# Layer 1 of a two-layer attention kernel: three engines held to the program's order, and the softmax, its bands and the contraction moved one to two columns later

## The chip, the core and the metric

The kernel runs on one NeuronCore of a Trainium2 chip. The metric is the device time of one execution in microseconds, as the median of repeated runs. A profile is one further execution, recorded by the hardware profiler; it is a little longer than the timed ones.

## What is computed

Two layers follow each other on a map of 8 images, 56 rows, 56 columns and 384 channels, all in 32-bit floats. Each adds to its input the result of local attention over 3 x 3 neighbours, after a group normalisation. Layer 1, which the change is about:

```python
a = x_map @ W_attn + b_attn                       # 6 heads x 9 weights for each pixel
a = softmax(a.reshape(B, H*W, heads, k*k), axis=-1)
v = x_map @ W_v + b_v
patches = stack([vp[:, i:i+H, j:j+W, :] for i in range(k) for j in range(k)], axis=3)
y = einsum('bpKhd,bphK->bphd', patches, a)        # weighted sum of 9 neighbours, by head
return y.reshape(B, H, W, C) @ W_proj + b_proj    # and x is added
```

## The kernel before

The images are taken in four pairs. A column is one image column of a pair: 2 x 56 rows, 112 pixels. Seven columns make a group, so that a pair has 8 groups and layer 1 has 32. Layer 0 runs first and takes some 2,340 us; its last tile is finished while layer 1 begins.

Layer 1 is one loop over steps (`layer1`, its loop at L932). Step `g*7 + m` handles column `m` of group `g`, and work of earlier groups beside it:

- `load` (L718) brings the group's input, 1176 KB, from DRAM by a SyncE transfer, into one of four buffers. `normed` (L728) normalises it on ScalarE into `xn`, two sets of 8 columns.
- `attend` (L769) projects 128 pixels at once on TensorE into a PSUM bank (the tiles called "bank"), 54 attention logits and 384 values. VectorE adds the biases: once into `lgt`, once into `v`. ScalarE issues the two stores of `v` to DRAM (`spread`). A tile of 128 pixels straddles two columns of 112, so 8 columns give 7 tiles, and every eighth column (`col % 8 == 0`) has no attend. Below that is a skipped column.
- `regroup` (L792) stores a group's logits to DRAM (`lgtab`, issued by ScalarE) and loads them back with pixels of one column on the partitions (`at`, issued by SyncE).
- `weigh` (L813) is the softmax: maximum and subtraction on VectorE, exp on ScalarE, sum and reciprocal on VectorE, multiplication by the reciprocal on GpSimd (L824).
- `move` (L826) shifts the weights by matrix products on TensorE (`pw`), copies them with nine ScalarE copies into `wz`, and writes them to DRAM (`ztab`, 496 KB, issued by ScalarE).
- `fetch` (L855) loads the patches of `v` (`vp`, two transfers of 945 KB) and the band matrices made of the weights (`z`, four transfers of 258 KB), all by SyncE, and queues jobs. The contraction jobs (`pc`, for each image four small blocks of row tiles) multiply patches by bands on TensorE, and ScalarE copies the sums into `yT`. The projection jobs (`po`, six of them) multiply by the output weights, and VectorE adds bias and input. The turns (`pt`, seven) transpose the result on TensorE, ScalarE copies it to `ot`, and SyncE stores it in two transfers.

Two calls of `jobs.run` in each step take one queued job each. `due` makes the first contraction job of a group wait until four steps after `fetch`.

The order on TensorE is fixed by hand: each matmul and transpose passes through `tc.keep_in_program_order` (L118 to L122), so that it is issued as the program has it. The order on the other engines is chosen by a scheduler when the kernel is built, from an estimate of when each instruction can start[...].

Of the kernel before, what the change touches and what calls it, by code (L numbers as in the profile page):

```python
# [15 lines left out]
def two_outlook_layers(  # L16
# [342 lines left out]
    def rows_to_patches(vp, table, px, r0, py, npy, sx):  # L359
        first = (px * (R + GAP) + GAP - MARGIN + r0) * sx * C  # L360
        nc.sync.dma_start(
            vp,
            bass.AP(
                table.tensor, table.offset + first, [[C, vp.shape[0]], [py * sx * C, npy], [1, C]]
            ),
        )
# [13 lines left out]
    def layer0(late, pools):  # L380
# [14 lines left out]
        def stats_chunk(pair, blk, i, alone):  # L395

            nm = f"{pair}_{blk}"
            if blk == 0 and i == 0:
                stats[pair] = stat.tile([P, NCH, IMG, NBLK, 6], F32, tag="st0", name=f"st0_{pair}")
            if i == 0:  # L400
                xts[pair, blk] = io.tile([P, NCH, XB, R], F32, tag="xt", name=f"xt_{nm}")
            xr, xt = xrs[pair, blk], xts[pair, blk]
            if alone:
                pt = bank(P, 0, XB * R).rearrange("p (m r) -> p m r", m=XB)
            else:
                pt = ps.tile([P, XB, R], F32, tag="t", name=f"pt_{nm}_{i}")
            for j in range(XB):
                transpose(pt[:, j, :], xr[:, j, i * P : (i + 1) * P], ident[:R, :R])
            nc.scalar.copy(xt[:, i], pt)
            for b in range(IMG):  # L410
                nc.vector.bn_stats(stats[pair][:, i, b, blk, :], xt[:, i, :, b * H : (b + 1) * H])
            if i == NCH - 1:
                nc.sync.dma_start(
                    xTs[pair][:, :, blk * XB * R : (blk + 1) * XB * R], xt.rearrange("p i m r -> p i (m r)")
                )
                del xrs[pair, blk], xts[pair, blk]
# [149 lines left out]
        def fetch_v(pair, px):  # L566

            vps[:] = [patch_tiles(f"0_{pair}_{px}", b) for b in range(IMG)]
            for b in range(IMG):
                rows_to_patches(vps[b], vtab0, px, b * H, PY0, NPY0, SX0)  # L570
# [139 lines left out]

    def layer1(pools, base, last_of_layer0, late_w):
        io = pools.enter_context(tc.tile_pool(name="io1", bufs=2))
# [4 lines left out]

        def load(g):  # L718
            pair, px = divmod(g, NPX)

            if g % 4 == 3:
                t = late_w.tile([P, NCH, T], F32, tag="xres", name=f"x1t_{g}")
            else:
                t = io.tile([P, NCH, T], F32, tag="x1t", name=f"x1t_{g}", bufs=3)
            nc.sync.dma_start(t, x1s[pair][px])
            x1ts[g] = t.rearrange("p i (m r) -> p i m r", m=PX)

        def normed(g, m0, m1):  # L728

            scale, bias = params1[g // NPX]  # L730
            first = g * PX
            cut = (first + m0) // SB * SB + SB
            for lo, hi in ((first + m0, min(cut, first + m1)), (cut, first + m1)):
                if lo >= hi:
                    continue
                to = xns[lo // SB % 2][:, :, lo % SB : lo % SB + hi - lo, :]
                for i in range(NCH):
                    for b in range(IMG):
                        rows = slice(b * H, (b + 1) * H)
                        nc.scalar.activation(  # L740
                            to[:, i, :, rows], x1ts[g][:, i, lo - first : hi - first, rows],
                            AF.Identity,
                            bias=bias[:, i, b : b + 1], scale=scale[:, i, b : b + 1],
                        )
# [5 lines left out]
        nc.sync.dma_start(wc_t[:, :, :NA1], wa1.rearrange("(i p) n -> p i n", p=P))  # L750
        nc.sync.dma_start(wc_t[:, :, NA1:], wv1.rearrange("(i p) n -> p i n", p=P))
# [8 lines left out]

        NZ = 4
        half_z = NPY1 * PY1 * ROW1
        zs1 = [
            zs[n // 2].rearrange("p n e -> p (n e)")[: SX1 * SY1, n % 2 * half_z : (n % 2 + 1) * half_z]
            .rearrange("p (n e) -> p n e", n=NPY1)
            for n in range(NZ)
        ]

        def attend(g, m):  # L769

            col = g * PX + m
            if col % SB == 0:
                return
# [5 lines left out]
            nc.vector.tensor_add(staged[-1][1][:, len(staged[-1][0])], pa[:, :NA1], ba_t)  # L779
            staged[-1][0].append(col // SB * NT + tile_no)  # L780
            v = work.tile([P, C], F32, tag="v", name=f"v_1_{col}", bufs=5)
            nc.vector.tensor_add(v, pa[:, NA1:], bv_t)
            for lo, n_col, row, n in parts_of(tile_no):
                c = col - col % SB + n_col
                spread(nc.scalar, vtab1, SX1, c % W, 1, row, v[lo : lo + n])
# [6 lines left out]
        def regroup(g):  # L792
# [3 lines left out]
            nc.scalar.dma_start(  # L796
# [7 lines left out]
            nc.sync.dma_start(  # L804
# [8 lines left out]
        def weigh(g):  # L813

            at = lgs[g]
            heads_last = [R, PX, K2, HEADS1]
            mx = work.tile([R, PX, HEADS1], F32, tag="mx", name=f"mx1_{g}")
            nc.vector.tensor_reduce(mx, at.rearrange("r x k h -> r x h k"), AX.X, ALU.max)
            nc.vector.tensor_tensor(at, at, mx.unsqueeze(2).to_broadcast(heads_last), ALU.subtract)
            nc.scalar.activation(at, at, AF.Exp)  # L820
            den = work.tile([R, PX, HEADS1], F32, tag="den", name=f"den1_{g}")
            nc.vector.tensor_reduce(den, at.rearrange("r x k h -> r x h k"), AX.X, ALU.add)
            nc.vector.reciprocal(den, den)  # L823
            nc.gpsimd.tensor_tensor(at, at, den.unsqueeze(2).to_broadcast(heads_last), ALU.mult)  # L824

        def move(g):  # L826
# [14 lines left out]
            for kj in range(K):  # L841
                dst = wz[:, kj * K * ROW1 : kj * K * ROW1 + PX * step].rearrange("r (m e) -> r m e", e=step)
                dst = dst[:, :, : K * ROW1].rearrange("r m (e h o) -> r e m h o", e=K, h=HEADS1)
                for e in range(K):
                    nc.scalar.copy(dst[:, e, :, :, 0], pw[:, e, :, kj, :])
            table = ztab1[g % NTAB]
            nc.scalar.dma_start(
# [5 lines left out]
            )  # L853

        def fetch(g, due):  # L855
# [5 lines left out]
            for b in range(IMG):  # L861
                rows_to_patches(vps[b], vtab1, px, b * H + MARGIN - 1, PY1, NPY1, SX1)
            for b in range(IMG):
                z, vp = zs1[(g * IMG + b) % NZ], vps[b]
                bands(
                    nc.sync, z, ztab1[g % NTAB], LINE1, SLOT1, ROW1, MARGIN - 1, GROUPS1,
                    b, PY1, NPY1,
                )

                def contract(t, b=b, z=z, vp=vp):  # L870
# [12 lines left out]
                    nc.scalar.copy(  # L883
# [9 lines left out]
            def project_out(half, j):  # L893
# [5 lines left out]
                nc.vector.scalar_tensor_tensor(  # L899
# [3 lines left out]
            def turn(m):  # L903
# [8 lines left out]
                nc.scalar.copy(fetch.ot[:, m - lo, :], pt)  # L912
                if m == hi - 1:
                    nc.sync.dma_start(
# [17 lines left out]
        for step in range(NG * PX + 4):  # L932
# [7 lines left out]
            if g < NG:  # L940
                attend(g, m)
# [3 lines left out]
            if m == 4 and g + 1 < NG:  # L945
                load(g + 1)
# [4 lines left out]
            jobs.run(base + step, 1)  # L951

            if g and m == 2:
                weigh(g - 1)
            if g and m == 3:
                move(g - 1)
                while not clear_bands.done:
                    jobs.run(None, 1)
                fetch(g - 1, base + step + 4)
        jobs.run(None, -1)  # L960
# [46 lines left out]
```

## Time and profile before

| | |
|---|---|
| time, median of 3 runs | 3582.99 us (3578.41 to 3585.44) |
| span of the profiled execution | 3610.8 us |
| mean granted TensorE clock | 0.978 of full speed |
| TensorE busy, 0 to 2340 us | 2275.6 us |
| TensorE busy, 2340 to 2411 us | 61.0 of 71 us |
| TensorE busy, 2411 to 3553 us (31 groups) | 1077.3 of 1142 us, clock 0.98 |
| TensorE busy, 3553 to 3611 us (after the last attend) | 46.7 of 58 us, clock 0.95 |

The page gives busy time by engine, then the same in 40 slices of the span as tenths, with the clock granted to TensorE. PE is TensorE's matmul, PEld its weight load, DVE is VectorE, ACT ScalarE, POOL GpSimd and SP SyncE; a "q" behind a name (ACTq, SPq) is the engine's issuing of transfers. In a list of waits each row says who waited for whom, how long in all, how often, and the longest. In the timeline a row has the start, the length, the engine, the line and operation, output and inputs, and in brackets the idle time before it with the engine or transfer that ended it. A busy TensorE still isn't at its peak, because matmuls are pipelined and their ends are modelled; so lengths here are taken from start to start.

### The profile page before, as it was taken

How to read it: one execution, taken by the hardware profiler on the slowest of the kernel's cores; microseconds unless marked ns; L12 is line 12 of the kernel's file. 1: busy time of each engine (PE TensorE's matmuls, PEld its weight loads, DVE VectorE, ACT ScalarE, POOL GpSimd, SP SyncE). 2: the span in 40 equal slices, each digit the busy share in tenths (PEclk: the TensorE clock that was granted, in tenths of full speed). 3: DMA queues.
4: the chain of work that ended last, by engine and by line, in shares of the span. 5: the costliest groups of instructions: out<-in, count | busy, mean ns of one | idle time of the engine just before them, and what ended most of it. 6: DMA issues, size and time to landing. Idle time of an engine off the chain costs nothing.

```text
span 3610.8 us, 72232 instructions
## 1 busy us (share of the span) xinstructions
PE 3460.6 (96%) x29078; PEld 2375.8 (66%) x29078; DVE 1914.9 (53%) x4648; ACT 1165.1 (32%) x2727; POOL 986.4 (27%) x1409
## 2 busy tenths in 40 slices
PE   4999999999999999999999999989999999999998
PEld 4667767777777777777767777655565565556555
DVE  3766666667666676667666666532222222222222
ACT  2333322332333333333222322232333433333332
POOL 2444334434444434443444444410000000000000
PEclk6999999999999999999999999999999999999999
DMA  9799988688886778887667777677778787777876
GB/s 294 202 285 292 267 265 257 226 249 263 267 271 208 263 238 254 261 258 262 204 208 241 218 223 231 222 252 188 207 200 220 206 226 196 199 218 198 219 196 159
DMA packets 692253, 840.73 MB, mean 233 GB/s; under 512 B 302222, under 2 KB 596174, under 8 KB 687822
## 3 DMA queue, kind: packets, MB, share of 16 engines
q1 hardware_dynamic: 329614, 576.00, 51.1%
q10 hardware_dynamic: 362304, 260.11, 27.5%
q8 instruction: 229, 3.75, 0.5%
q14 instruction: 106, 0.87, 0.1%
HBM read 514.32 MB, written 321.66 MB: 232 GB/s over the span
## 4 chain that ended last, share of the span: by engine, by line
PE 78%; DMA 16%; DVE 2%; ACT 1%; issue 1%; POOL 1%; ACTq 0%; SPq 0%; POOLq 0%; DVEq 0%
PE bank L119 44%; PE po L119 15%; PE pc L119 11%; DMA ztab<-wz 5%; PE pw L119 4%; DMA z<-ztab 3%; DMA lgtab<-lgt 2%; PE pt L122 2%; DMA at<-lgtab 1%; DMA xr<-in_x 1%; PE bank L122 1%; DMA vtab<-v 1%; DMA x1t<-x 1%; DMA xT<-xt 1%; DMA vp<-vtab 1%
## 5 line engine op out<-in xcount | busy, mean ns | idle before, releaser
L119 PE MATMUL bank<-wa_t,xn 128*112 128x288 f32 x4032 | 1083.6, 408 | 2.2 <-ACT xn L471 2.2
L119 PEld LDWEIGHTS bank<-wa_t,xn 128*112 128x112 f32 x4032 | 691.9, 177 | 253.1 <-issue 31.9
L510 POOL TENSOR_TENSOR at<-at,den 112x972 f32<-112x972 f32 x224 | 504.9, 2254 | 1226.6 <-DVE den L509 1181.7
L119 PE MATMUL po<-yT,wo_t 128*128 128x448 f32 (+1 forms) x2304 | 823.7, 497 | 5.4 <-DVE x1t L621 4.8
L119 PEld LDWEIGHTS po<-yT,wo_t 128*128 128x128 f32 x2304 | 435.3, 192 | 296.2 <-issue 192.2
L119 PE MATMUL pc<-z,vp 121*32 121x49 f32 (+1 forms) x17664 | 490.0, 255 | 50.6 <-DMA z<-ztab 23.1
L119 PEld LDWEIGHTS pc<-z,vp 121*32 121x32 f32 (+1 forms) x17664 | 444.2, 131 | 127.5 <-issue 91.8
L119 PE MATMUL bank<-wc_t,xn 128*128 128x438 f32 x1176 | 485.7, 549 | 3.8 <-DMA wc_t<-in_wv 2.6
L486 DVE TENSOR_REDUCE mx<-bank 112x36 f32<-112x324 f32 x672 | 327.1, 487 | 299.5 <-PE bank L119 292.9
L119 PE MATMUL bank<-wv_t,xn 128*128 128x384 f32 x1176 | 418.6, 492 | 0.0
L824 POOL TENSOR_TENSOR at<-at,den 112x378 f32<-112x378 f32 x32 | 30.2, 945 | 1142.4 <-DVE den L823 704.8
L487 DVE TENSOR_TENSOR at<-bank,mx 112x324 f32<-112x324 f32 x672 | 328.5, 489 | 21.1 <-DVE mx L486 0.5
L491 ACT ACTIVATE at<-at 112x972 f32<-112x972 f32 x224 | 227.1, 1014 | 331.7 <-DVE at L487 307.9
L119 PEld LDWEIGHTS bank<-wc_t,xn 128*128 128x128 f32 x1176 | 216.3, 193 | 177.9 <-issue 167.2
L740 ACT ACTIVATE xn<-x1t,bias,scale 128x168 f32<-128x168 f32 (+4 forms) x498 | 213.6, 503 | 322.1 <-DMA x1t<-x 227.9
L119 PEld LDWEIGHTS bank<-wv_t,xn 128*128 128x128 f32 x1176 | 219.5, 191 | 139.5 <-issue 18.6
L899 DVE SCALAR_TENSOR_TENSOR x1t<-po,bo_t,x1t 128x448 f32<-128x448 f32 (+1 forms) x192 | 120.1, 626 | 339.6 <-PE po L119 339.6
L555 ACT COPY wt<-pw 112x120 f32<-112x120 f32 x224 | 58.0, 259 | 662.1 <-PE pw L119 577.5
L533 POOL TENSOR_TENSOR pre<-at,at 112x108 f32<-112x108 f32 (+1 forms) x440 | 238.0, 541 | 115.0 <-DVE wt L556 100.6
L779 DVE TENSOR_TENSOR lgt<-bank,ba_t 128x54 f32<-128x54 f32 x196 | 41.1, 210 | 417.2 <-PE bank L119 417.1
L503 DVE TENSOR_TENSOR d<-at 112x432 f32<-112x432 f32 x224 | 141.1, 630 | 196.9 <-ACT at L491 196.9
L600 ACT COPY yT<-pc 128x294 f32<-128x294 f32 x256 | 103.3, 408 | 372.1 <-PE pc L119 318.8
(81 smaller groups left out, 2845.4 us busy)
## 6 DMA issues: line engine op xcount, KB each, us to landing
z<-ztab SPq DMA_DIRECT2D x64, 2352.0 KB
vp<-vtab SPq DMA_DIRECT2D x64, 1536.0 KB
ztab<-wt ACTq DMA_DIRECT2D x336, 183.8 KB
vp<-vtab SPq DMA_DIRECT2D x64, 945.0 KB
xT<-xt SPq DMA_DIRECT2D x56, 672.0 KB
xin<-xT ACTq DMA_DIRECT2D x56, 672.0 KB
xres<-xT SPq DMA_DIRECT2D x32, 1176.0 KB
x1t<-x SPq DMA_DIRECT2D x32, 1176.0 KB
```

The costliest lines, as they stand in the source:

```text
L119: tc.keep_in_program_order(nc.tensor.matmul(*args, **kwargs))
L122: tc.keep_in_program_order(nc.tensor.transpose(*args, **kwargs))
L486: nc.vector.tensor_reduce(mx[:, pi, :], pl.rearrange("r q a -> r a q"), AX.X, ALU.max)
L487: nc.vector.tensor_tensor(at[:, pi], pl, mx[:, pi, :].unsqueeze(1).to_broadcast([R, K2, PH]), ALU.subtract)
L491: nc.scalar.activation(at, at, AF.Exp, scale=SCALE0)
L503: nc.vector.tensor_add(d4, at[:, :, 0:4], at[:, :, 4:8])
L510: nc.gpsimd.tensor_tensor(at, at, den.unsqueeze(2).to_broadcast([R, K, K2, PH]), ALU.mult)
L533: nc.gpsimd.tensor_tensor(dst, terms[0], terms[1], ALU.add)
L555: nc.scalar.copy(mid[:, 0 : E0 : E0 - 1, :], pw[:, 0 : E0 : E0 - 1, :])
L600: nc.scalar.copy(yT[:, :, :, b, rows_of], pc.rearrange("p i n y m -> p i m (n y)"))
L740: nc.scalar.activation(to[:, i, :, rows], x1ts[g][:, i, lo - first : hi - first, rows], AF.Identity, bias=bias[:, i, b : b + 1], scale=sca ...
L899: nc.vector.scalar_tensor_tensor(res, po[:, :n], bo_t[:, j : j + 1], res, ALU.add, ALU.add)
```

## The change

An object `InOrder` wraps VectorE, ScalarE and SyncE within layer 1, so that what they are given there keeps the program's order like the matmuls. The loop is rearranged by hand to suit. The softmax goes from column 2 to column 3 (and ahead of the second job), the move from 3 to 4, the patch loads and the jobs' due time from 3 to 5, the band loads, now a function `fetch_bands`, from 3 to 6. The stores of `v` come after the second job. The input's load goes from column 4 to column 1 of the group before, for which there are five buffers instead of four. The fifth is a half of the bands' memory, so there are three sets of bands instead of four. The loop runs three steps further.

It is meant to take the order out of the scheduler's estimate, and to give the transfers of weights and bands more columns in which to arrive.

```diff
+    class InOrder:
+        def __init__(self, engine):
+            self.engine = engine
+        def __getattr__(self, name):
+            op = getattr(self.engine, name)
+            return lambda *args, **kwargs: tc.keep_in_program_order(op(*args, **kwargs))
...
     def layer1(pools, base, last_of_layer0, late_w):
+        vector, scalar, sync = (InOrder(e) for e in (nc.vector, nc.scalar, nc.sync))
...
+        NZ = 3
+        half = NPY0 * PY0 * ROW0 // 2
+        halves = [z.rearrange("p n e -> p (n e)")[:, n * half : (n + 1) * half] for z in zs for n in range(2)]
...
-            if g % 4 == 3:
+            if g % 5 == 3:
                 t = late_w.tile([P, NCH, T], F32, tag="xres", name=f"x1t_{g}")
+            elif g % 5 == 4:
+                t = halves[3][:, : NCH * T].rearrange("p (i t) -> p i t", i=NCH)
             else:
                 t = io.tile([P, NCH, T], F32, tag="x1t", name=f"x1t_{g}", bufs=3)
-            nc.sync.dma_start(t, x1s[pair][px])
+            sync.dma_start(t, x1s[pair][px])
...
-        NZ = 4
...
-            for lo, n_col, row, n in parts_of(tile_no):
-                c = col - col % SB + n_col
-                spread(nc.scalar, vtab1, SX1, c % W, 1, row, v[lo : lo + n])
+            return lambda: [
+                spread(scalar, vtab1, SX1, (col - col % SB + n_col) % W, 1, row, v[lo : lo + n])
+                for lo, n_col, row, n in parts_of(tile_no)
+            ]
...
+        def fetch_bands(g):
+            for b in range(IMG):
+                bands(
+                    sync, zs1[(g * IMG + b) % NZ], ztab1[g % NTAB], LINE1, SLOT1, ROW1, MARGIN - 1,
+                    GROUPS1, b, PY1, NPY1,
+                )
...
-        for step in range(NG * PX + 4):
+        for step in range(NG * PX + 7):
             g, m = divmod(step, PX)
             jobs.run(base + step, 1)
...
-            if g < NG:
-                attend(g, m)
+            store = attend(g, m) if g < NG else lambda: None
+
+            if g and m == 3:
+                weigh(g - 1)
+            jobs.run(base + step, 1)
             if g and m == 0:
                 regroup(g - 1)
                 stage(g)
-            if m == 4 and g + 1 < NG:
-                load(g + 1)
+            store()
             if m == 6 and g + 1 < NG:
                 normed(g + 1, 0, 3)
             if m == 0 and 0 < g < NG:
                 normed(g, 3, PX)
-            jobs.run(base + step, 1)
-
-            if g and m == 2:
-                weigh(g - 1)
-            if g and m == 3:
+            if m == 1 and g + 1 < NG:
+                load(g + 1)
+            if g and m == 4:
                 move(g - 1)
+            if g and m == 5:
                 while not clear_bands.done:
                     jobs.run(None, 1)
                 fetch(g - 1, base + step + 4)
+            if g and m == 6:
+                fetch_bands(g - 1)
```

All other calls of `nc.vector`, `nc.scalar` and `nc.sync` within layer 1 become calls of the wrapped engines. In layer 0 the transfers that store the transposed first pair are held to the program's order too.

## The prediction

> **What bounds the kernel now.** I read the engine table and the slices of the page first, then the waits of TensorE in layer 1, then its timeline, then clock windows.
>
> ```profile
> PE 3460.6 (96%) x29078; PEld 2375.8 (66%) x29078; DVE 1914.9 (53%) x4648; ACT 1165.1 (32%) x2727; POOL 986.4 (27%) x1409
> PEclk6999999999999999999999999999999999999999
> ```
>
> TensorE (PE) is the bound and its order is fixed in both kernels, so only its idle gaps and its clock can change. Layer 0's instructions stand in the same order on every engine in both builds; the change begins at about 2340 us. These are the waits of PE from 2411 us (the first softmax result of layer 1) to the end: us in total, times, longest.
>
> ```profile
> PE pw L119 <- POOL at L824: 27.4, 16, 3.7
> PE pc L119 <- DMA z<-ztab: 23.1, 12, 4.5
> PE pc L119 <- issue: 12.7, 6, 3.3
> PE pc L119 <- ACT yT L883: 4.8, 8, 0.8
> PE pt L122 <- ACT ot L912: 1.6, 3, 1.2
> ```
>
> The row "pw" is the move of the softmax weights waiting for their last multiplication; "pc" is the contraction waiting for its bands (the "issue" gaps too: each ends 5.1 to 5.3 us after a band load was issued). Together 69.6 us in 32 groups. Each long gap costs twice: windows around the wait at 3302, with the granted clock in the column before the DMA share:
>
> ```profile
> 3301.00:3305.00 4.00, 1.62 (x11) 1.03 (x9) 2.61 (x7) 1.37 (x4) 0.95 (x1) 1.00 1.04 207
> 3305.00:3309.00 4.00, 4.00 (x9) 1.90 (x8) 0.00 (x0) 1.47 (x11) 0.00 (x0) 0.57 1.10 255
> 3309.00:3313.00 4.00, 4.00 (x13) 2.00 (x12) 1.36 (x3) 0.00 (x0) 0.00 (x0) 1.00 1.10 320
> ```
>
> Windows of 20 us over 2411 to 3600 add up to 29.4 us of clock lost. There are 16 gaps of 2.1 us or more, and none of the shorter ones is followed by a drop: 1.85 us for each such gap. So layer 1 loses 69.6 + 29.4 = 99 us after 2411. That is the most that can be won, and waits can be added.
>
> The timeline of PE gives the lengths of the pieces (start, length, start of the next):
>
> ```profile
> 2774.03 0.49 PE L122 MATMUL pt<-ident,x1t 128*112 128x128 f32 x3
> 2774.45 1.61 PE L119 MATMUL pc<-z,vp 90*64 90x56 f32 x48
> 2775.99 2.47 PE L119 MATMUL bank<-wc_t,xn 128*128 128x438 f32 x6
> 2778.30 0.49 PE L122 MATMUL bank<-ident,x1t 128*112 128x128 f32 x3
> 2778.73 1.26 PE L119 MATMUL pc<-z,vp 90*64 90x56 f32 x36
> ```
>
> From start to start: turn (pt) 0.42, or 0.33 ahead of pw or po; contraction of two row tiles 1.54, of the last two 1.19; attend (bank) 2.31, after po 2.21. From other rows alike: po 2.25 and 1.70, pw 0.65.
>
> **What the skill says.** The Trainium skill, "TensorE: Matmul & The Clock Gate", Part 1: the clock falls to half after an idle window of 3413 ns, and windows run freely. The trace agrees on the half and the length (0.57 over 4 us), though here gaps of 2.2 us suffice. "PSUM — Partial Sum Buffer", Engine vs sequencer instructions: ScalarE and VectorE are strict FIFO. The trace agrees: at 2990 VectorE stands 6.43 us before the softmax maximum while a finished bank waits. "DMA: Bandwidth & Descriptors", Issuing engines are not separate DMA queues: transfers issued by ScalarE and SyncE interleave on the same 16 engines. The trace agrees: the weight write took 9.1 and 9.8 us from issue to band issue in the last two groups, with no input load near it, and 12.1 us in the mean from the third group on (timeline of the queues).
>
> **Part 1, softmax one column later.** In the steady state of before, the logits' store follows the attend of column 0, the maximum starts 6.0 to 10.3 us after that store, and maximum to pw takes 4.6 us (maximum to subtraction 0.95, exp at 1.52, sum at 2.07, reciprocal at 2.94, multiplication 3.60 to 4.55). PE has 10.2 us of work in between when one of the columns 1 to 3 is skipped (one column in eight has no attend), else 12.5; hence the 27.4 us. In the changed order about 20.8 us of PE work lie between, so the load no longer matters. But VectorE's order now puts the maximum behind the two additions of column 3's attend, and pw comes after the turn, the contraction, the attend and the turn of column 4. Let E be the end of column 3's attend on PE. The first addition starts at E+0.20, the second 0.13 later, the maximum 0.47 after that: E+0.80. pw can start at E+0.80+4.60 = E+5.40. PE arrives at E+0.42+1.54+2.31+0.33 = E+4.60. **A wait of 0.8 us in an ordinary group.** Where column 4 is skipped, PE arrives at E+2.4: 3.0 us. Where column 3 is skipped, the maximum follows column 2's additions, PE has 6.3 us, no wait. Each skip hits 4 groups in 32. Group 1 has no turns yet and waits 1.6; in the last, exp stands on ScalarE behind two copies of the contraction, 1.1. Sum: 21 x 0.8 + 4 x 3.0 + 1.6 + 1.1 = 31.5 us. Behind the waiting sum on VectorE stand only column 4's additions, whose bank is done at E+4.3, about when the reciprocal is: free. Behind exp on ScalarE stand a turn's copy, two stores and two contraction copies, done by E+5.1, before PE wants them: free.
>
> **Part 2, bands and contraction later.** From pw to the bands' arrival: 2.4 us to the issue of the weight write (median; nine copies on ScalarE), its latency, and 5.4 us from the band issue. With 12.0 us of latency that is 19.8. In before PE's work from pw to the contraction is 17.9 with a skip among three columns, 20.3 without; with a spread of 1.6 us the expected wait is (3/8) x 1.9 + (5/8) x 0.44 = 1.0 us, 31 us in 31 groups; measured 35.8 with the first group's 4.5. The sum holds. In the changed order PE does pw, 1.19, turn, six po, three turns and four attends: 24.05, or 21.8 in the half of the groups with a skip. The latency is the unknown. The input load (1176 KB, within 4 us of the write in most groups) goes away from it, but the two patch loads (945 KB each), which stood 4 to 11 us ahead of it, now follow an output store on SyncE and are issued about 3 us behind it. Bounds: 9.1 (nothing beside it) and 14.9 (longest seen). I take 13 with a spread of 1.7: arrival 20.9, wait 0.43 where a column is skipped, 0.05 elsewhere; about 9 us in all with a few slow ones. At the start, pw and four attends (9.6 us) cover a chain of 16 to 17: 7 us. At the end 15.1 us of work cover 17.5: 2.4. Sum 18.4 us.
>
> **Part 3, the rest.** Five inputs and the earlier load: the load stands five columns ahead of its first reader instead of two; the ScalarE waits for it in before (10 us each) end no chain of PE: nothing. Three sets of bands: the set a load overwrites was last read three columns before: nothing. ScalarE's order puts the nine copies and the write ahead of the last two contraction copies; where column 5 is skipped PE waits 1.1, 4 groups: 4.4 us. The 6.4 us of other ScalarE waits stay. On SyncE the 1.5 MB patch load of layer 0's last tile now goes ahead of layer 1's first input and weights, for which PE already waits 2.6 us at 2356; 1.5 MB at the 276 GB/s of that stretch is 5.6 us, of which I take 5.
>
> **Sum.** Afterwards: softmax 31.5, bands 18.4, ScalarE 10.8, clock 9 long gaps (4 skips, start, end, 3 slow bands) x 1.85 = 16.7: 77.4 against 99, and 5 more at the start: -16.6 us. 3583 - 17 = 3566. By halves, with 7 of the 16 long gaps on the softmax and 9 on the bands: softmax 31.5 + 7.4 instead of 27.4 + 13, about nothing; bands 18.4 + 9.3 instead of 35.8 + 16.6, which is the gain.
>
> **Rivals.** (a) Cleaner: the weight write falls to 9.5 us without the input load beside it. No steady band waits (-9), three drops fewer (-5.6), no new ScalarE wait (-4.4), 2 instead of 5 at the start: 3544. For it: the last two groups. Against it: patch loads carry more bytes than the input did. (b) Slower: patch loads, output and vector stores stretch the write to 15.5 us: arrival 23.4, waits 1.75 and 0.40, 34 us instead of 9, seven more drops 13: +38, 3604. For it: 13.7 to 14.9 us occurred in four groups with far fewer bytes behind the write. Against it: the write has a lead of about 3 us. (c) No change: a latency near 14 and a start that costs all of 5.6 leave 3583 within 7.
>
> **Chances.** Mine 0.50, (a) 0.20, (b) 0.18, (c) 0.12. Mine spreads over 3550 to 3582, so faster by over 0.2% (under 3576) 0.64, same 0.15, slower (over 3590) 0.21. The range 3538 to 3601 takes in (a), (c) and most of (b).
>
> **What would show it.** Right: pw waits in nearly every group of about 0.8 us, four of 3 us where column 4 is skipped; VectorE no longer waits for the logits' load; ScalarE no longer for inputs; band waits under 12 us after the first group; write latency near 13; about nine clock drops. Wrong: no pw waits (then the additions didn't hold the maximum), or a write latency over 15 with band waits in half the groups.

## The result, and the profile after

In the comparison that the prediction was made for, the changed kernel took 3629.41 us (median of 4 runs, 3621.87 to 3638.53) against 3581.19 us for the kernel before in the same set of runs. The ratio is 1.0135, with a 95% interval of 1.0109 to 1.0161: slower, where 3566 us and faster had been forecast. Beside three later sets of runs the same kernel gave 1.0093 (1.0063 to 1.0123), 1.0074 (1.0061 to 1.0088) and 1.0055 (1.0036 to 1.0075). Its own median stayed between 3629 and 3637 us. The kernel before gave medians of 3581 to 3612 us in the different sets, and no run here says why; so every ratio below is taken against the runs of the kernel before in the same set, and the loss is told as 0.5 to 1.4%.

First the engine table of the page and the granted clock in 40 slices, for the changed kernel:

```profile
PE 3477.6 (96%) x29078; PEld 2390.1 (66%) x29078; DVE 1918.5 (53%) x4648; ACT 1176.5 (32%) x2727; POOL 986.2 (27%) x1409
PEclk6999999999999999999999999999999999999997
```

TensorE does the same 29078 instructions and is busy for 17 us longer than before. The last slice of the clock shows 7 instead of 9, and after the first softmax move the clock record loses 52.3 us instead of 29.9. Next the main waits of TensorE from 2411 us to the end (us in total, times, longest; a wait of 2.5 us for `xn` and 0.5 us of others are left out):

```profile
PE pc L119 <- DMA z<-ztab: 26.5, 9, 5.1
PE pw L119 <- POOL at L838: 25.6, 26, 2.9
PE pc L119 <- issue: 11.4, 4, 5.9
PE pc L119 <- ACT yT L721: 2.1, 3, 1.4
PE po L119 <- ACT yT L721: 1.9, 4, 0.5
```

The softmax wait ("pw") is now short and regular, as forecast: 0.61 to 0.64 us in 21 groups, 2.9 us in the four where column 4 is skipped. The wait for the bands ("pc" for "z", the "issue" rows too) should have fallen from 35.8 to 18.4 us. It is 37.9 us in 13 groups, and the two longest waits, 5.1 and 5.9 us, are in the last two groups.

One steady group shows why. The softmax move of this group starts at 2889.52. The weight write is issued by ScalarE (timeline of ScalarE's issues):

```profile
2891.49 0.32 ACTq L721 DMA_DIRECT2D ztab<-wz  x1
```

SyncE's timeline around it (start, length over all issues of the row, line, operation, number of issues; the first row holds two stores that lie 13.6 us apart):

```profile
2881.24 13.98 SPq L721 DMA_DIRECT2D out<-ot  x2
2895.33 2.73 SPq L721 DMA_DIRECT2D vp<-vtab  x2
2898.16 8.55 SPq L721 DMA_DIRECT2D z<-ztab  x4
```

And TensorE's (the bracket is the idle time before the row):

```profile
2914.89 2.82 PE L119 MATMUL pc<-z,vp 90*64 90x56 f32 x48 [3.29 <-issue]
```

The bands are issued 6.7 us after the weight write, not 13 us. The write itself is faster still: its last packet has moved 3.3 us after its issue (median of the groups, from the packet records; 11.4 us in the kernel before). SyncE comes to the bands only after an output store and both patch loads. In the kernel before it stood waiting for the weight write in all 32 groups, in the changed one in 6 (waits of SyncE, before and changed):

```profile
SPq L308 <- DMA ztab<-wz: 308.8, 32, 14.8
SPq L721 <- DMA ztab<-wz: 26.3, 6, 13.9
```

But from the band issue to the contraction it takes 16.7 us, not 5.4 us. Right ahead of the bands SyncE has issued the output store and the patch loads. In the kernel before, a group at the same place looked like this on SyncE and on TensorE:

```profile
2897.75 0.34 SPq L725 DMA_DIRECT2D x1t<-x  x1
2907.68 1.83 SPq L308 DMA_DIRECT2D z<-ztab  x4
```

```profile
2912.92 1.61 PE L119 MATMUL pc<-z,vp 90*64 90x56 f32 x48 [1.99 <-DMA z<-ztab]
```

There the bands were issued 10 us after the last other load, and 5.2 us sufficed.

In the changed kernel the four band loads also leave one by one: the fourth left 8.2 us after the first here (median 10.7 us, before 1.3), when the first patch load had landed. This is not what makes the bands late. In the last group the fourth left after 4.2 us and the last band packet moved 17.6 us after the first issue; in the 26th these were 12.1 and 18.2 us.

The end of the layer is a story of its own. Windows over the last band wait, with the granted clock in the column before the DMA share:

```profile
3585.00:3589.00 4.00, 0.91 (x6) 0.42 (x4) 0.57 (x1) 0.48 (x1) 0.00 (x0) 1.00 1.08 165
3589.00:3593.00 4.00, 1.23 (x24) 1.26 (x25) 0.00 (x0) 0.00 (x0) 0.00 (x0) 0.71 0.72 132
3593.00:3597.00 4.00, 4.00 (x65) 3.55 (x63) 0.00 (x0) 1.44 (x4) 0.00 (x0) 0.50 0.07 23
3597.00:3601.00 4.00, 4.00 (x61) 3.45 (x59) 0.00 (x0) 1.57 (x4) 0.00 (x0) 0.50 0.48 153
3601.00:3605.00 4.00, 4.00 (x45) 3.50 (x44) 0.00 (x0) 1.80 (x5) 0.00 (x0) 0.50 0.00 0
3605.00:3609.00 4.00, 4.00 (x8) 1.83 (x7) 0.38 (x1) 0.34 (x1) 0.00 (x0) 0.66 0.41 129
```

The half clock begins at 3590.65, 1.1 us before the wait ends, and lasts 17.07 us, though TensorE is then busy without a break. The same happens around the end of the wait of 5.1 us, from 3556.5 on. Each costs about 8 us on top of its wait: half of what lies behind the wait's end.

To place the loss, layer 1 is cut at three starts of the move (pw): the last of layer 0, the first of layer 1, and the 30th of its 32. "Gaps" are the idle times of TensorE over 0.2 us, "clock" is time multiplied by the missing share of the clock. Worked out from the timeline and the clock record of each profile:

| stretch | before, two profiles | changed, four profiles |
|---|---|---|
| start | 70.5, 71.0 us (gaps 10; clock 2) | 78.1 to 80.9 us (gaps 12 to 13; clock 2 to 3) |
| first to 30th pw | 1086.1, 1084.3 us (gaps 62, 57; clock 27, 31) | 1078.1 to 1091.5 us (gaps 54 to 60; clock 29 to 44) |
| 30th pw to the end | 113.2, 109.8 us (gaps 8, 6; clock 3, 2) | 131.1 to 133.7 us (gaps 15 to 16; clock 18 to 20) |

Because pw stands one column later, about 5.5 us of work come into the start, and some 4 us leave each of the other two stretches. In the means of the profiles the start then costs 3 us more of gaps and clock. The steady groups come out even (3 us more of gaps and clock, 4 us less of work). The end takes 21 us longer: about 8 more of gaps and 17 more of clock, less 4 of moved work. That is 28 us in all. The medians of the three later sets differ by 25 to 33 us, those of the first by 48; the other 20 us of the first set are in no profile, and stay open.

### The profile page after: what moved, and what is told of

Its sections match the earlier page's. It is cut to its first block, busy times and chain, and to the rows that moved or that the text cites. A ratio compares the mean times of both kernels' runs of the same rounds, so it can differ in the third digit from the quotient of the medians.

```text
span 3627.0 us, 72273 instructions
## 1 busy us (share of the span) xinstructions
PE 3477.6 (96%) x29078; PEld 2390.1 (66%) x29078; DVE 1918.5 (53%) x4648; ACT 1176.5 (32%) x2727; POOL 986.2 (27%) x1409
## 4 chain that ended last, share of the span: by engine, by line
PE 82%; DMA 10%; DVE 3%; POOL 1%; ACT 1%; issue 1%; SPq 0%; ACTq 0%; POOLq 0%; DVEq 0%
PE bank L119 46%; PE po L119 17%; PE pc L119 11%; DMA z<-ztab 5%; PE pw L119 5%; PE pt L122 2%; DMA xr<-in_x 1%; DMA lgtab<-lgt 1%; PE bank L122 1%; DMA vp<-vtab 1%; POOL at L838 1%; DMA xT<-xt 1%; DVE den L721 1%; DVE mx L721 1%; DMA x1t<-x 1%
## 5 line engine op out<-in xcount | busy, mean ns | idle before, releaser
L119 PE MATMUL pc<-z,vp 121*32 121x49 f32 (+1 forms) x17664 | 500.4, 257 | 45.9 <-DMA z<-ztab 26.5
L119 PEld LDWEIGHTS pc<-z,vp 121*32 121x32 f32 (+1 forms) x17664 | 454.3, 133 | 121.5 <-issue 70.4
L119 PE MATMUL bank<-wc_t,xn 128*128 128x438 f32 x1176 | 494.6, 558 | 8.8 <-ACT xn L721 8.8
L721 DVE SCALAR_TENSOR_TENSOR x1t<-po,bo_t,x1t 128x448 f32<-128x448 f32 (+1 forms) x156 | 97.6, 625 | 262.8 <-PE po L119 262.8
L721 ACT ACTIVATE xn<-x1t,bias,scale 128x168 f32<-128x168 f32 (+4 forms) x402 | 168.2, 500 | 163.0 <-issue 55.5
```

What stands on the lines that cost most here:

```text
L119: tc.keep_in_program_order(nc.tensor.matmul(*args, **kwargs))
L721: return lambda *args, **kwargs: tc.keep_in_program_order(op(*args, **kwargs))
```

## The experiments

The first theory (Q): the bands are late because they stand behind the patch loads in SyncE's queue. Its rival (S): all loads share the same engines, so only the bytes count, in whatever order. The second: the short pw waits come from the maximum standing behind column 3's additions. Later: where the loss sits, and what the clock costs by itself.

**The softmax one column earlier.**

```diff
-            if g and m == 3:
+            if g and m == 2:
                 weigh(g - 1)
```

> The changed kernel with one edit: the softmax of a group is written at column 2 instead of column 3, so its maximum stands behind column 2's additions on VectorE. Theory (the pw waits come only from the maximum standing behind column 3's additions): the 26 pw waits of 25.6 us go, and with them the four gaps of 2.87 us and their clock drops (4 x about 1.85), 33 us in all; the band waits, whose chain starts at pw, stay at 38 us. 3629 - 33 = 3596 us. Rival (a gap closed at pw opens again at the contraction, because the band loads stand behind patch loads whose start does not follow pw): pw waits gone, but band waits grow from 38 to 55 to 65 us, 3615 to 3625 us.

Measured: 3635.96 us, ratio 1.0084 (1.0060 to 1.0109). The median lies within the 3629 to 3637 us of the changed kernel. All 26 pw waits are gone, so their cause is shown. But nothing was won. The band waits stay at 38.2 us, and 19.8 us of waits for ScalarE's copies of the contraction ("pc" for "yT", 18 times) have come in. The rival had the direction right; it came on a third way, through ScalarE instead of the bands.

**One patch load ahead of the move.**

```diff
             if g and m == 4:
+                fetch_patches(g - 1, 0)
                 move(g - 1)
...
-            for b in range(IMG):
-                rows_to_patches(sync, vps[b], vtab1, px, b * H + MARGIN - 1, PY1, NPY1, SX1)
+            fetch_patches(g, 1)
```

> The changed kernel with one edit: the first of the two patch loads of a group (945 KB) is issued one column earlier, ahead of the move, so that only one patch load stands ahead of the band loads in SyncE's queue. Theory Q (the bands are late because they stand behind two patch loads in one queue): from band issue to contraction 15.4 to 17.2 us becomes 10 to 12.5, more than the 2.0 to 3.6 us that TensorE waits; steady band waits go from 38 us to under 10, and about 13 clock drops with them: 3629 - 28 - 20 = 3581 us. Rival S (all loads share the 16 engines, and only the bytes in flight around the bands count): the bands still take 14 us or more, since the first patch load now runs beside the weight write and delays that: waits over 25 us, 3615 to 3635 us. The pw waits stay at about 25 us under both.

Measured: 3577.29 us, ratio 0.9918 (0.9895 to 0.9941). The waits of the move and of the contraction from 2411 us on:

```profile
PE pw L119 <- POOL at L838: 30.4, 27, 4.2
PE pc L119 <- ACT yT L721: 1.2, 2, 1.0
PE pc L119 <- DMA z<-ztab: 0.8, 2, 0.4
```

37.9 us of band waits have become 0.8, and the clock lost after the first pw falls from 52.3 to 19.7 us. SyncE's timeline in the group at the same place:

```profile
2883.84 0.32 SPq L721 DMA_DIRECT2D vp<-vtab  x1
2895.70 0.33 SPq L721 DMA_DIRECT2D out<-ot  x1
2896.12 0.39 SPq L721 DMA_DIRECT2D vp<-vtab  x1
2896.84 4.34 SPq L721 DMA_DIRECT2D z<-ztab  x4
```

The first patch load leaves 12 us earlier; the second still follows the output store. TensorE reaches the contraction 22.0 us after pw and finds the bands there.

**Both.** The two edits together.

> The changed kernel with both edits: softmax written at column 2, first patch load ahead of the move. If both theories hold the gains add: 3629 - 33 - 48 = 3548 us, 35 us below the kernel before, with layer-1 waits under 25 us. If the waits only move from pw to the contraction: 3590 us or more. If the engines are shared whatever the queue (rival S): about 3596, as with the softmax alone.

Measured: 3558.53 us, ratio 0.9869 (0.9844 to 0.9894): faster than both kernels. With the bands on time the earlier softmax does pay, half a per cent over the patch load alone. Of 22 us of waits that are left, these are the contraction's:

```profile
PE pc L119 <- ACT yT L721: 13.7, 9, 4.7
PE pc L119 <- DMA z<-ztab: 1.6, 1, 1.6
```

**The bands issued by GpSimd.**

```diff
                 bands(
-                    sync, zs1[(g * IMG + b) % NZ], ztab1[g % NTAB], LINE1, SLOT1, ROW1, MARGIN - 1,
+                    nc.gpsimd, zs1[(g * IMG + b) % NZ], ztab1[g % NTAB], LINE1, SLOT1, ROW1, MARGIN - 1,
```

> The changed kernel with one edit: the band loads are issued by GpSimd instead of SyncE; the patch loads stay where they are, with the same bytes at the same time. Theory Q (order in SyncE's queue): the bands no longer stand behind the patch loads: from band issue to contraction 7 to 10 us instead of 15.4 to 17.2, band waits under 10 us, 3575 to 3590 us. Rival S (the 16 engines are shared by bytes, whatever queue the transfers stand in): still 14 us or more, band waits 30 us or more, 3620 to 3635 us. The pw waits stay at about 25 us under both, unless the issue on GpSimd holds up its multiplication.

Measured: 3594.21 us, ratio 0.9965 (0.9952 to 0.9979). Band waits are 5.4 us, if the "issue" row counts for them. The same bytes, issued 0.9 us sooner (medians) from another queue, and the waits are nearly gone: what stood ahead of them in SyncE's queue mattered. But the row of issues (number, KB each, median us from issue to landing) says 12.4 us, above the 7 to 10 that pure Q expected:

```profile
z<-ztab POOLq DMA_DIRECT2D x128, 258.4 KB, 12.4
```

So S is true in part. Beside the patch loads the bands go slower (last packet 15.6 us after the first issue, against 7.1 in the kernel before), and only what was ahead of them in the queue falls away.

**The bands ahead of the patch loads, in the same queue.**

```diff
             if g and m == 5:
+                fetch_bands(g - 1)
                 fetch(g - 1, base + step + 4)
-            if g and m == 6:
-                fetch_bands(g - 1)
```

> The changed kernel with one edit: the four band loads of a group are written ahead of its two patch loads, so that on SyncE they stand in front of the patch loads instead of behind them. Same bytes, same queue, other order. Theory Q (order in SyncE's queue): the bands land 5 to 8 us after their issue, about pw + 15; the patch loads follow them and land by pw + 20, before the contraction at pw + 22 to 24: band waits under 5 us, and the ratio to before is that of the kernel with one patch load moved ahead, 0.989 to 0.995. Rival S (the bytes around the bands count, in whatever order): band and patch loads are in flight together as before, 20 us or more of waits for bands or patches remain, ratio over 1.002. A third outcome: the patch loads, now held back by the wait for the weight write, become the last to land, and TensorE waits for patches in many groups: ratio 0.998 to 1.015.

Measured: 3579.81 us, ratio 0.9945 (0.9929 to 0.9961). The waits of the move and those for transfers from 2420 us on:

```profile
PE pw L119 <- POOL at L838: 30.9, 27, 5.3
PE pc L119 <- DMA vp<-vtab: 6.8, 5, 5.2
```

No band wait is left, with the same bytes in the same queue. The bands stand one column earlier here and are issued 1.8 us sooner (medians), which is little beside the 9.1 us by which they now land sooner after their issue. Patches are waited for five times, 5.2 us of it in the first group.

The packet records make the queue visible. Band packets are the only ones of 840 bytes in SyncE's queue, and the packets of the weight write the only ones of 504 bytes. Medians over the 32 groups in us, worked out from the records: the first two columns count from the issue of the weight write, the last two from the first band issue.

```
kernel                      write's last   bands    first band   last band
                            packet         issued   packet       packet
before                         11.4         12.2       0.9          7.1
changed                         3.3          6.1       9.1         17.7
one patch load ahead of move    3.5          4.9       5.6         13.5
both edits                      5.1          6.6       3.3         11.2
bands ahead of patches          3.3          4.3       2.1          8.6
```

In the changed kernel 9.1 us pass before the first byte of the bands moves. With one 945 KB load less in front it is 3.5 us less.

**The order alone, at the columns of before.** Only the wrapping of VectorE, ScalarE and SyncE is added to the kernel before.

```diff
     def layer1(pools, base, last_of_layer0, late_w):
+        vector, scalar, sync = (InOrder(e) for e in (nc.vector, nc.scalar, nc.sync))
```

> The kernel before with one edit: VectorE, ScalarE and SyncE of layer 1 held to the program's order, no column moved. On SyncE the store of the second half of the output then stands ahead of the patch loads, as in the changed kernel, and the patch loads ahead of the bands. If the held order is what makes the bands late (Q), they need 14 us or more from issue, while TensorE has only 17.9 to 20.3 us of work from pw to the contraction: waits of 3 to 6 us in nearly every group, over 100 us, ratio 1.03 or more. If the held order is harmless by itself and the loss came from the later columns, the ratio is 0.995 to 1.008.

Measured: 3912.73 us, ratio 1.0868 (1.0849 to 1.0887). The size was as Q expected, the cause was not. The contraction follows the band issue by 4.8 to 6.0 us wherever it waits for the bands. The time goes elsewhere (the three largest waits from 2420 us on):

```profile
PE bank L119 <- ACT xn L721: 102.3, 26, 5.9
PE pc L119 <- ACT yT L721: 90.3, 30, 7.8
PE pw L119 <- POOL at L837: 47.3, 30, 4.7
```

In program order the input load stands behind the band loads on SyncE, leaves mostly 12 to 17 us after the weight write, and ScalarE stands in front of its normalisation (175.9 us of waits for that load) with the contraction's copies behind it. This points to the earlier input load, with its fifth buffer, as what makes the held order bearable; no run added them alone.

**The shift alone, without the held order.** The changed kernel with the three engines left to the scheduler.

```diff
-        vector, scalar, sync = (InOrder(e) for e in (nc.vector, nc.scalar, nc.sync))
+        vector, scalar, sync = nc.vector, nc.scalar, nc.sync
```

> The changed kernel with one edit: the columns stay where the change put them, but VectorE, ScalarE and SyncE are left to the scheduler. It puts the maximum ahead of column 3's additions (so no pw waits: 25 us less) and the patch loads ahead of the output store, but the input load (1176 KB) between patch loads and bands. If what counts is when the patch loads start (Q), they start early again, as in the kernel before, and the bands have only the input load ahead of them: band waits under 15 us, ratio 0.985 to 0.995. If three loads ahead of the bands make them as late as two did: band waits over 38 us, ratio 1.005 or more.

Measured: 3605.07 us, ratio 1.0018 (1.0006 to 1.0030). Neither branch was right. The patch loads do leave early again and the bands are waited for once. In their place stand 41 waits of the contraction for ScalarE:

```profile
PE pc L119 <- ACT yT L900: 52.9, 41, 3.0
PE pc L119 <- DMA z<-ztab: 6.4, 1, 6.4
```

One of them, on VectorE and then on ScalarE, ahead of a contraction that waits 2.81 us until 3032.88:

```profile
3030.06 0.83 DVE L832 TENSOR_REDUCE mx<-at 112x42 f32<-112x378 f32 x1 [5.96 <-DMA at<-lgtab]
3030.93 0.55 DVE L795 TENSOR_TENSOR v<-bank,bv_t 128x384 f32<-128x384 f32 x1
```

```profile
3031.85 0.48 ACT L929 COPY ot<-pt 112x384 f32<-112x384 f32 x1 [7.51 <-DVE v L795]
3032.38 0.44 ACT L900 COPY yT<-pc 128x336 f32<-128x336 f32 x1
```

The scheduler put the maximum ahead of the additions; it waits for the logits' load; the store of v waits on ScalarE for the addition; the contraction's copy waits behind the store. Holding the order does away with this chain (VectorE's waits for the logits' load fall from 171.6 us here to 8.4 in the changed kernel).

**Both edits, and exp behind the contraction of its column.** To see where the 13.7 us of ScalarE waits come from, exp and what follows it are written after the second job of column 2.

```diff
             if g and m == 2:
                 weigh(g - 1)
             jobs.run(base + step, 1)
+            if g and m == 2:
+                weigh2(g - 1)
```

> The kernel with both edits (softmax at column 2, first patch load ahead of the move), and the softmax cut in two: maximum and subtraction stay at column 2, but exp, sum, reciprocal and multiplication are written after the contraction of column 2, so that on ScalarE exp no longer stands ahead of the contraction's copies. If the remaining ScalarE waits of the kernel with both edits (13.7 us in front of contractions) come from exp waiting there for the subtraction, they fall under 5 us, with two or three clock drops less: ratio about 0.005 under 0.987. If they come from other work on ScalarE, nothing changes (0.984 to 0.990). If exp now comes too late for pw, pw waits return: 0.990 or more.

Measured: 3562.29 us, ratio 0.9879 (0.9864 to 0.9895), the same as without the split within the intervals. The waits went up, to 20.3 us in 18 places. That exp alone holds up the copies is refuted; what does is left open.

**The kernel before, and the changed one, once more.**

> The kernel before once more, unedited, for a second profile, since the execution profiled first took 31 us more than the median of its timed runs. If that profile is typical of layer 1, the second one again shows about 70 us of gaps and 29 us of clock lost after the first softmax result. If it was a bad one, both sums are lower, by up to 31 us together, and the changed kernel's loss against it is that much clearer.

> The changed kernel once more, unedited, beside the runs that follow, since two sets of runs of the kernel before differ by 25 us (3583 and 3608). If the loss belongs to the program and not to the place where it was measured, the ratio to before is again 1.011 to 1.016, with band waits near 38 us, pw waits near 26 us and 45 to 55 us of clock lost in layer 1. If a good part of it was chance, the ratio is under 1.008.

> The changed kernel, unedited, as the partner of the next run on the same chip: 1.006 to 1.016 of the kernel before, and two stretches of 13 to 17 us at half clock after the last two band waits of 5 to 6 us.

Measured: the second profile of before (span 3602.4 us) has 62.9 us of gaps and 32.5 us of clock after the first pw, close to the 69.7 and 29.9 of the first, so the first was a fair picture of layer 1. Its execution took 3612.7 us, within the runs of the kernel before in the later sets but 31 us above its own set's median; the profiled execution of the changed kernel took 3628.93 us, no more than its median. The repeats of the changed kernel gave 1.0093 and 1.0074, with 69 and 75 us of gaps and 64 and 47 us of clock. The loss is the program's, but smaller than in the first comparison.

**A filler in the last two waits.** The changed kernel, with 13 matmuls whose result nobody reads ahead of the contractions of the last two groups.

```diff
                 def contract(t, b=b, z=z, vp=vp):
+                    if g >= NG - 2 and b == 0 and t == 0:
+                        d = ps.tile([P, 4 * R], F32, tag="o", name=f"warm_{g}")
+                        tokens = xns[0].rearrange("p i m r -> p i (m r)")
+                        for n in range(13):
+                            matmul(d, wo_t[:, 0, :P], tokens[:, 0, : 4 * R], start=True, stop=True)
```

> The changed kernel with one addition: ahead of the contractions of the last two groups TensorE does 13 matmuls of 448 columns (about 4.8 us) whose result nobody reads; they fill the two long band waits and move no other work. Theory C (the idle wait lowers the clock, and in the last groups it stays low for four to five windows): the two stretches of 13 to 17 us at half clock vanish, and about 14 to 17 us with them, 0.4 to 0.5% under the unedited kernel beside it. Rival (the clock is low there because the work of the last groups is thin): the stretches stay, and the time is the same or 1 to 4 us longer. Third: the band waits end so late that no clock is saved beyond the first window: 3 to 7 us.

Measured: 3633.09 us, ratio 1.0078 (1.0064 to 1.0092), as the partner's 1.0074. Both stretches at half clock are gone. But the filler took 9.94 us each time, not 4.8: the estimate had taken six records of a projection for six matmuls, and the profile writes two records for each of these (26 for the 13 of the filler). It was longer than the waits of 5.2 and 6.4 us, and gave back what the clock saved. A filler of the right length follows below.

**The filler at the right length, and the bands mended in the last two groups only.** The first has 6 matmuls instead of 13. The second moves one patch load ahead of the move, as above, but for groups 31 and 32 alone:

```diff
+            if g and m == 4 and g - 1 >= NG - 2:
+                fetch_patches(g - 1, 0)
```

> The changed kernel, unedited, as the partner of the next two runs on the same chip: 1.006 to 1.012 of the kernel before; from the softmax move of the 30th group to the end 131 to 135 us.

> The changed kernel with one edit, in the last two of 32 groups only: the first patch load is issued one column earlier, ahead of the move; the other 30 groups stay as they are. If the end is where the loss to the kernel before sits, the stretch from the 30th softmax move to the end falls from 132 to 113 us, as in the kernel that repairs all groups, and the time falls by 16 to 22 us, to 1.001 to 1.004 of the kernel before. If the steady groups carry the loss, the time falls by 6 us or less.

> The changed kernel with 6 instead of 13 filler matmuls (0.76 us each by the run before, 4.6 us) ahead of the contractions of the last two groups, whose result nobody reads: shorter than the waits of 5.2 and 6.4 us, so nothing moves but the clock. If the half clock after these waits is itself the cost, its 17 us stretches vanish and the end shrinks by 10 to 17 us, to 1.003 to 1.006 of the kernel before. If the waits are what costs and the clock only follows, 0 to 5 us.

Measured, on one chip: unedited 3637.45 us, ratio 1.0055 (1.0036 to 1.0075), end stretch 131.1 us. Filler 3627.78 us, 1.0042 (1.0026 to 1.0059), end 126.0 us. Bands mended 3616.90 us, 1.0017 (0.9999 to 1.0034), end 116.0 us. TensorE's timeline of the kernel with the filler, at the last group:

```profile
3579.84 4.68 PE L119 MATMUL warm<-xn,wo_t 128*128 128x448 f32 x12
3585.79 1.61 PE L119 MATMUL pc<-z,vp 90*64 90x56 f32 x48 [1.28 <-issue]
```

And at the same place in the changed kernel:

```profile
3591.77 2.82 PE L119 MATMUL pc<-z,vp 90*64 90x56 f32 x48 [5.86 <-issue]
```

After the filler the contraction takes 1.61 us, in the changed kernel after its wait 2.82. The clock lost in the end stretch falls from 18.1 to 6.0 us. The bands don't come sooner: the contractions start 16.4 and 16.5 us after the band issue (unedited 16.4 and 15.8). The median falls by 9.7 us, though the intervals of the two ratios overlap. The end stretch of the profile falls by only 5.1 us, in part because a pw wait of 3.5 us has come in at the last group. With the bands mended in two groups of 32 the median falls by 20.6 us, the end stretch by 15.1, and no difference to the kernel before can be told. So the end carries the loss against the kernel before, as the cut by stretches said.

## Why the prediction was wrong

The terms of the sum, in us. Measured are the waits of the changed kernel and its clock record after the first pw:

| term | predicted | measured |
|---|---|---|
| softmax waits | 31.5 | 25.6 |
| band waits, start | 7 | 0 |
| band waits, steady groups | 9 | 26.9 |
| band waits, end | 2.4 | 11.0 |
| ScalarE waits | 10.8 | 7.0 |
| clock | 16.7 | 52.3 |
| sum | 77.4 | 122.8 |

Before had 99, so 24 us are lost here, and some 3 at the start. Of the 45 us between the two columns, about 35 are in the first 30 groups (bands 18; clock 32.4 instead of 8 gaps x 1.85 = 14.8) and about 27 at the end (bands 9, clock 18), less 17 that softmax, ScalarE and the first group took off. Against the kernel before the first 30 groups are even; there the forecast gain did not come.

**Part 1, softmax: right.** The chain E + 5.40 against E + 4.60 gave 0.8 and 3.0 us; measured 0.62 and 2.9. The group with no turns waits 1.1 instead of 1.6, and the wait of 1.1 forecast for the last group did not come. That the logits' load hardly counts any more was right (VectorE waits 8.4 us for it instead of 112). The run with the softmax at column 2 shows the cause.

**Part 2, bands: the step that failed.** The prediction took "13 with a spread of 1.7" for the weight write, called this "the unknown", and added "5.4 us from the band issue" as a known. Both were wrong, in opposite directions. The write, up to the band issue, takes 4.8 to 8.4 us, below the lower bound of 9.1. Even that is not the write's own time, which is 3.3 us: the bands leave when SyncE has issued what stands ahead of them. In the kernel before, the patch loads were issued 8.1 and 5.0 us ahead of the write (medians), and in most groups the input load ran beside it too; now the patch loads follow it and the input load is gone. No run parts the two, but in the last two groups of before, with no input load near, the write still took 7.8 and 9.2 us, so the patch loads had a large part.

The 5.4 us became 15.4 to 17.2 us where TensorE waited, and the sum, pw + 20.9, came out there at pw + 23.6 to 25.7. (With a lead of 0.9 us and a spread of 1.7 a normal spread gives a wait of 0.3 us rather than 0.43; this is too small to matter.)

The prediction had even said that the patch loads "are issued about 3 us behind" the write (3.8 in most groups). It charged them to the write, which is in ScalarE's queue, and not to the bands behind them in SyncE's own. The 5.4 us was measured with nothing right ahead in the queue (0.9 us to the first packet) and did not carry over. The Trainium skill, "DMA: Bandwidth & Descriptors", Two DMAs through the same engine are not ordered, says that the descriptors (the single pieces of a transfer) within one queue of one DMA engine start in order. The trace agrees: 9.1 us to the first band packet behind the store and the two patch loads. The prediction drew from that page only that the issuers share the engines.

**The end: the same step.** "At the end 15.1 us of work cover 17.5: 2.4" used the same 5.4. Between pw and the contraction lie four attends in a steady group, two in the 31st and none in the last; the prediction had no wait for the 31st. Measured were 5.1 and 5.9 us. The run that mends these two groups alone takes 20.6 us off.

**Clock: the size was off.** Nine gaps at "1.85 us for each such gap" were expected. There were 13 of 2.1 us or more. Up to the 30th pw the clock lost 32.4 us with 10 of them, 3.2 us for each if all is put down to them, though shorter waits were followed by drops too. The two over 5 us came with 17.07 us at half clock, 8.5 us of lost clock each. The short filler shows that the clock falls there because TensorE stands idle, and that the half clock by itself is worth some of the 21 us: 10 by the medians, 5 by the one profile.

**Start: the mechanism right, the size smaller.** Five us were expected for the patch load of layer 0 ahead of the first input. The waits for the first input and its weights are longer there (4.6 and 1.8 us instead of 2.6 and 1.2), but others shrank, and the stretch has 2 to 3 us more of gaps. A new wait of 2.5 us for xn follows the first pw. The 7 us of band wait at the first group did not come: no patch load stood right in front of those bands (5.6 us from issue), so the whole chain took 14.1 us instead of 16 to 17, and TensorE spent part of that on the new wait for xn and at half clock (3.41 us from 2423.3).

**Part 3.** The ScalarE wait where a column is skipped came as told, four times, at 0.5 instead of 1.1 us. Buffers and input load show no cost, as told: ScalarE's waits for inputs (227.9 us from 2440 us on in the kernel before) are gone. That the new positions carry the held order was not seen; without them the order alone costs 8.7%.

**Rivals.** Rival (b), slower, had the arrival (pw + 23.4) and the band waits (34 us) nearly right, by a wrong way, a write of 15.5 us. Nothing in its working asked what stood in front of the bands.

## What to carry to other kernels

The time from a transfer's issue to its landing belongs to its place in the queue: before carrying it over, list what the new order puts in front of it on the same issuer, and add those bytes to this transfer rather than to its neighbour in another queue. When work is moved later in a software pipeline, work out the last groups apart, since there nothing is left to hide a wait. Holding three engines to a written order takes one set of waits away and makes others. The price of one part depends on the others: the order alone cost 8.7%, the new positions alone 0.2%, both together 0.5 to 1.4%.

## What the runs showed of the hardware that was not expected

The half clock after a long wait can far outlast the wait. In the profiles here it lasted 3.41, 6.83, 10.24, 13.65 or 17.07 us, multiples of 3.41. All those of 17.07 us are in the last two groups, where after the wait come contractions with narrow outputs (64 x 56) and turns, without idle time. Full clock was back 1.4 and 3.1 us after the wide projections (128 x 448) began, at 3572.23 and 3604.62 in the changed kernel. (10.24 us, and once 13.65, came elsewhere too: with the order alone, the positions alone, and the bands ahead of the patches.) With the filler in front, the same narrow work ran at full clock. The Trainium skill, "TensorE: Matmul & The Clock Gate", Part 1, gives a return to full clock after about 3.4 us of sustained work; these stretches of busy TensorE do not fit that. That narrow work cannot lift the clock, though it can keep it, would fit, but no run tried it apart.

Short gaps have no sharp limit either: waits of 1.4 and 1.5 us were followed by drops of 3.41 us in the changed kernel, one of 2.15 us by none.

Bands issued by GpSimd moved in packets of 4200 bytes for the most part, those issued by SyncE in packets of 840. In the run with GpSimd both queues moved at once: on average 170 KB of bands and 101 KB of patches in 1.5 us of one group (2910 to 2918 us).
